# Where a scan's result is added up: row directions through TensorE and ScalarE, column directions on VectorE but later

## The chip, the cores and the metric

The kernel runs on one core of one Trainium2 chip. The metric is the device time of one execution in microseconds; lower is better. A core has five engines that each run their own queue of instructions in order: TensorE (PE, with its weight loads shown as PEld), VectorE (DVE), ScalarE (ACT), GpSimd (POOL) and SyncE (SP, which here only issues DMAs). They meet through semaphores.

## The reference

Two layers on an input of 4 images of 48 x 48 positions with 128 channels, all in float32. The part that matters here is the four-direction selective scan of the first layer:

```python
x0 = xc.reshape(B, d, L)
x1 = jnp.transpose(xc, (0, 1, 3, 2)).reshape(B, d, L)
xs = jnp.stack([x0, x1, x0[..., ::-1], x1[..., ::-1]], axis=1)
...
def step(h, inp):
    dt_l, u_l, B_l, C_l = inp
    dA = jnp.exp(dt_l[..., None] * A)
    h = h * dA + (dt_l * u_l)[..., None] * B_l[:, :, None, :]
    y = jnp.einsum('bkdn,bkn->bkd', h, C_l)
    return (h, y)
...
ys = ys + Ds.reshape(1, K, d, 1) * xs
y = ys[:, 0] + ys[:, 2][..., ::-1]
y1 = ys[:, 1] + ys[:, 3][..., ::-1]
y = y + jnp.transpose(y1.reshape(B, d, W, H), (0, 1, 3, 2)).reshape(B, d, L)
```

There are d = 256 inner channels and 16 states each; direction k = 0 goes along rows, 1 along columns, 2 and 3 are these backwards. The four results are added up. A layer normalisation, a gate and a projection follow. The second layer is an attention over the 2304 positions of each image and then a spectral filter ("stu"): 16 fixed filters `phi` are convolved with the sequence and mixed by matrices.

## The kernel before

**Stages.** The images are worked one after another. For each image there is a scan stage, and then a stage with epilogue (normalisation, gate, projection), attention and the next image's prologue (input projection, depthwise 3 x 3 filter). Ahead of the first image the prologue runs alone, with `weights` (loading and preparing the second layer's constants) threaded between its tasks. The spectral filter of image b runs on TensorE during the scan stage of image b + 1; that of the last image runs alone at the end, in another form. Image 0's scan stage has in its place `mixture`, which prepares the filter's matrices.

**The order is written out by hand**: the scheduler is off, and every engine runs its instructions in the order in which the Python code emits them.

**The scan stage.** `scans` runs over 192 units: 24 chunks (4 directions x 6 chunks of 384 positions), for each the 2 halves h of the inner channels and 4 groups q of states. A unit's tile `s` is 128 partitions (32 channels x 4 states) x 4 x 384. The life of unit u, one step of the loop per unit:

- `enter` (L517): s = dt*u times B, on VectorE for 5 units of 8 and on GpSimd for 3.
- `decay` (L526): ScalarE computes exp(dt*A) into one of the slots of `ring` in PSUM (4 slots for images 1 to 3). `fill`, called ahead of each scan, issues as many decays as there are free slots. Other short uses of PSUM (L438, L441, L509) take slots of the same ring.
- `scan` (L533): four scans a unit on VectorE; each frees its slot.
- `times_c` (L543): s times C, on GpSimd, in the next step.
- `sum_c` (L551): TensorE sums the 4 states of a channel with the matrix `csum` and accumulates the four q in one PSUM tile `ch.y`. It is emitted at the end of a step, for the two units of two and three steps before.
- `add_y` (L561, L563), one step after the last `sum_c` of a chunk's half: y is added to the image's sum `yaccs` (tiles `ya`, 128 x 48 x 48). In image 0, `sum_c` lets TensorE add the old content of `ya` to the same PSUM tile through an identity matrix (L554), and ScalarE copies the result back to `ya` (L561). In images 1 to 3 VectorE adds y to `ya` (L563). `in_order` gives the view of `ya` for a chunk: contiguous for row directions (even k), with a stride of 48 for column directions (odd k). `ch.y` has one buffer.

Between the four scans of a step, `more` emits work of the filter on TensorE by a budget of matmul columns (a share of the stage's total), so that its matmuls are spread evenly over the steps. In the filter (`stu`), three convolutions a filter (L1207) go through two PSUM banks, `cx` and `cy`; ScalarE copies them out (L1223, L1227, L1230, L1231), and L1273 multiplies by the mixing matrices. Each bank is written again only when its copy is done.

**The constants.** `weights` computes the differences of the filters, `fc` (L913 to L917), on 16 partitions x 1408 elements with three VectorE operations, and ScalarE's queue stores them to `fd`. They lie between the first tasks of the prologue, in which GpSimd computes a power (L243) for the normalisation that VectorE then applies (L245).

Of the kernel before, what the change touches and what calls it, by code (L numbers as in the profile page):

```python
# [10 lines left out]
ALU = mybir.AluOpType  # L11
# [13 lines left out]
G4, DL, C4, Q4 = 4, 32, 4, 4  # L25
# [35 lines left out]
def hybrid_kernel(ctx: ExitStack, tc: tile.TileContext, a: dict, out: bass.AP):  # L61
# [3 lines left out]
    nc = tc.nc  # L65
# [431 lines left out]
    class Unit:  # L497
# [47 lines left out]
        def sum_c(self, ps):  # L545

            ch = self.ch
            if self.q == 0:
                ch.y = ps.tile([P, 512], F32, tag="y", name=f"y{self.name}")
            for g in range(G4):  # L550
                nc.tensor.matmul(ch.y[g * DL:(g + 1) * DL, :CS], csum, self.s[:, g], start=(self.q == 0),  # L551
                                 stop=(self.q == Q4 - 1))
            if ch.b == 0 and self.q == Q4 - 1:
                nc.tensor.matmul(ch.y[:, :CS], ident, in_order(yaccs[ch.b][self.h], ch.k, ch.lo, CS), start=False,  # L554
                                 stop=True, skip_group_check=True)

        def add_y(self):
            ch = self.ch
            v = in_order(yaccs[ch.b][self.h], ch.k, ch.lo, CS)
            if ch.b == 0:  # L560
                nc.scalar.copy(v, ch.y[:, :CS].rearrange("p (r w) -> p r w", w=v.shape[2]))  # L561
                return
            nc.vector.tensor_tensor(v, v, ch.y[:, :CS].rearrange("p (r w) -> p r w", w=v.shape[2]), ALU.add)  # L563
# [53 lines left out]
    def scans(b, chunks, preps, front, sp, back, ring, finish, work, work_cols):  # L617

        units = [Unit(ch, h, q) for ch in chunks for h, q in quads]
        total = len(chunks) * CHUNK_COLS + work_cols  # L620
        done = [0]

        def more(share):

            while done[0] < share * total:
                cols = next(work, None)
                if cols is None:
                    break
                done[0] += cols

        def enter(s):

            if s + 2 < len(units) and units[s + 2].pool:
                units[s + 2].enter(sp.s, ring)
            if 0 <= s + 1 < len(units) and not units[s + 1].pool:
                units[s + 1].enter(sp.s, ring)

        wanted, issued = [], [0]

        def fill(left=0):  # L640

            while wanted and ring.free:
                wanted.pop(0).spread(ring)
            while len(ring.free) > left and issued[0] < G4 * len(units):
                i = issued[0]
                issued[0] += 1
                units[i // G4].decay(i % G4, ring)

        def scan(s, g):
            fill()  # L650
            units[s].scan(g, ring)

        def spread(s):
            if s < len(units) and not units[s].pool:
                wanted.append(units[s])

        def prepare(s):

            ci, j = divmod(s, len(quads))
            for c in range(ci + 1, ci + 5):  # L660
                if c < len(chunks) and 0 <= s - len(quads) * c + LEAD[c % 2] < STEPS[c % 2]:
                    done[0] += next(preps[c]) or 0

        def refill(s, i):

            if 0 <= s < len(units) and s // len(quads) + 1 < len(chunks):
                u, nxt = units[s], chunks[s // len(quads) + 1]
                if u.h == NH - 1:
                    nxt.fetch(i + u.q, front)

        pending = []
        spread(0)
        fill(len(ring.free) - 1)
        enter(-2)
        enter(-1)
        spread(1)
        fill(1)
        for i in range(3 if units[0].ch.b else 0):
            done[0] += next(work)
        for s in range(len(units) + 2):  # L680
            real = s < len(units)
            enter(s)
            prepare(s)
            if real:
                scan(s, 0)
            more((s + 0.25) / len(units))
            next(finish, None)
            if 1 <= s <= len(units):
                units[s - 1].times_c(s >= len(units) - (units[0].ch.b == 0))
            if real:  # L690
                scan(s, 1)
            if pending:
                pending.pop().add_y()
            prepare(s)
            more((s + 0.5) / len(units))
            next(finish, None)
            spread(s + 2)
            if real:
                scan(s, 2)
            more((s + 0.75) / len(units))  # L700
            next(finish, None)
            prepare(s)
            if real:
                scan(s, 3)
            refill(s - 2, Q4)
            refill(s + 1, 0)
            if s >= 2 and units[s - 2].q % 2:
                units[s - 3].sum_c(back.psy)
                units[s - 2].sum_c(back.psy)
                done[0] += 2 * CS  # L710
                if units[s - 2].q == Q4 - 1:
                    pending.append(units[s - 2])
            more((s + 1) / len(units))
            next(finish, None)
        for u in pending:
            u.add_y()
        for _ in work:
            pass
# [167 lines left out]
    def weights(one):  # L886

        def load(name, shape, src):  # L890
            t = one.tile(shape, F32, name=name)
            nc.scalar.dma_start(t, src)
            return t

        lg = load("lg", [P, NF], a["log_weights"].partition_broadcast(P))
        gu = load("gu", [P, NF], a["gumbel"].partition_broadcast(P))
        sg = load("sg", [P, KF], a["sigma"].partition_broadcast(P))
        ph = load("ph", [KF, 2, 2, LF + P + 1], a["phi"])
        mu = load("mu", [P, NF, 3, C], a["M_u"].rearrange("i j d e -> d i j e"))
        for i in range(6):  # L900
            yield
        hard, wts = [one.tile([P, NF], F32, name=n) for n in ("hard", "wts")]
        m = one.tile([P, 2], F32, name="m")

        nc.vector.tensor_add(lg, lg, gu)
        nc.vector.tensor_reduce(m[:, 0:1], lg, AX.X, ALU.max)
        nc.vector.tensor_scalar(lg, lg, m[:, 0:1], None, ALU.subtract)
        nc.scalar.activation(lg, lg, AF.Exp)
        yield

        fc = one.tile([KF, 3, 2, LF + P], F32, name="fc")
        n = LF + P
        nc.vector.tensor_copy(fc[:, 0], ph[:, :, 0, :n])  # L913
        yield
        nc.vector.tensor_sub(fc[:, 2], ph[:, :, 1, 1:], ph[:, :, 0, :n])
        yield
        nc.vector.tensor_sub(fc[:, 1], ph[:, :, 1, :n], ph[:, :, 0, :n])  # L917
        nc.scalar.dma_start(fd, fc)
        yield
        nc.vector.tensor_reduce(m[:, 0:1], lg, AX.X, ALU.add)  # L920
        nc.vector.reciprocal(m[:, 0:1], m[:, 0:1])
        nc.vector.tensor_scalar_mul(lg, lg, m[:, 0:1])
        nc.vector.tensor_reduce(m[:, 0:1], lg, AX.X, ALU.max)
        nc.vector.tensor_scalar(hard, lg, m[:, 0:1], None, ALU.is_equal)
        nc.vector.memset(m[:, 1:2], 1.0)
        yield
        for i in range(NF):

            nc.vector.tensor_tensor(hard[:, i:i + 1], hard[:, i:i + 1], m[:, 1:2], ALU.mult)
            nc.vector.tensor_tensor(m[:, 1:2], m[:, 1:2], hard[:, i:i + 1], ALU.subtract)  # L930
        nc.vector.tensor_sub(wts, hard, lg)
        nc.vector.tensor_add(wts, wts, lg)
        yield

        quarter = one.tile([P, KF], F32, name="quarter")
        nc.vector.memset(quarter, 0.25)
        nc.gpsimd.tensor_tensor(sg, sg, quarter, ALU.pow)
        mum = one.tile([P, NF, 3, C], F32, name="mum")
        nc.vector.tensor_scalar_mul(mum[:, NF - 1], mu[:, 0], wts[:, 0:1])
        for i in range(1, NF):  # L940
            nc.vector.tensor_scalar_mul(mum[:, NF - 1 - i], mu[:, i], wts[:, i:i + 1])
            nc.vector.tensor_tensor(mum[:, NF - 1 - i], mum[:, NF - 1 - i], mum[:, NF - i], ALU.add)
            yield
        nc.scalar.dma_start(mud, mum)
        for i in range(NF):
            nc.vector.tensor_scalar_mul(ws[:, :, i], sg, wts[:, i:i + 1])
        zero = one.tile([P, 4, 1], F32, name="zero")
        nc.vector.memset(zero, 0.0)
        nc.scalar.dma_start(ud[:, :, 0:1], zero)
# [817 lines left out]
```

## Time and profile before

| | us |
|---|---|
| median of 3 runs | 5428.56 (5426.13 to 5433.8) |
| profiled execution | 5427.03 |
| its span, first to last instruction | 5425.3 |
| scans of image 0 | 111.9 to 1059.3 |
| scans of image 1 | 1295.4 to 2250.8 |
| scans of image 2 | 2486.6 to 3442.2 |
| scans of image 3 | 3677.9 to 4633.2 |
| granted TensorE clock, mean (scan stage of image 0) | 0.926 (0.73) |

Times in the profile are microseconds from the first instruction of one profiled execution, unless marked ns. A group of instructions is one source line on one engine with its tiles, out<-in. A waits row names the engine and line that sat idle and, after the arrow, who ended the wait. A matmul in float32 stands in the profile as two instructions, and the ends of matmuls are modelled.

The busy share of the span in 40 equal slices, in tenths (9 is 90% or more), shows the alternation of the stages: four scan stages with VectorE at 9, and between them stretches in which TensorE leads.

```profile
PE   4555555599999999998899999898899999989999
...
DVE  8999999856999999856999999658999999423211
ACT  3666666546777766456776766457777666432111
POOL 2999999713989999605999999407998999201100
PEclk7777777799999999999999999999999999999999
```

### The profile page before, as it was taken

Reading aid. Unit: us, or ns where it says so; the run is one execution under the profiler, and the core shown is the slowest. Engines: PE = TensorE matmul, PEld = TensorE weight load, DVE = VectorE, ACT = ScalarE, POOL = GpSimd, SP = SyncE. Lnnn points to the kernel's source line nnn. Section 1 sums busy time; section 2 is a strip of 40 time slices with the busy share of each in tenths; the row PEclk is TensorE's granted clock in tenths of the full one; section 3 lists DMA queues with packets and bytes.
Section 4 is the critical chain, followed back from the end, with each engine's and each line's share of the span. In section 5 each row is a group of like instructions: output and inputs, shape, how many; then the busy total and the mean of one; then the engine's idle time right before and its main releaser. Section 6 shows DMA issues by size and latency. Waiting matters only on the chain. (4 is left out here: it accounts for less than half of the span.)

```text
span 5425.3 us, 71267 instructions
## 1 busy us (share of the span) xinstructions
PE 4658.1 (86%) x23372; PEld 3120.5 (58%) x23372; DVE 4324.9 (80%) x5309; ACT 3210.7 (59%) x6846; POOL 3656.8 (67%) x1881
## 2 busy tenths in 40 slices
PE   4555555599999999998899999898899999989999
PEld 2222222255666666645666666656666667559987
DVE  8999999856999999856999999658999999423211
ACT  3666666546777766456776766457777666432111
POOL 2999999713989999605999999407998999201100
PEclk7777777799999999999999999999999999999999
DMA  4444454404877777406787787227777777136543
GB/s 138 154 162 155 160 171 160 128 27 145 247 260 253 252 260 244 146 31 204 237 264 249 243 272 247 88 78 211 248 246 260 248 260 238 38 83 153 151 142 91
DMA packets 732185, 996.11 MB, mean 184 GB/s; under 512 B 108969, under 2 KB 580649, under 8 KB 731753
## 3 DMA queue, kind: packets, MB, share of 16 engines
q1 hardware_dynamic: 725992, 988.26, 57.6%
q10 hardware_dynamic: 5824, 3.30, 0.3%
q8 instruction: 187, 3.06, 0.2%
q14 instruction: 182, 1.48, 0.1%
HBM read 873.03 MB, written 118.31 MB: 183 GB/s over the span
## 5 line engine op out<-in xcount | busy, mean ns | idle before, releaser
L533 DVE TENSOR_TENSOR_SCAN s<-ring,s 128x385 f32<-128x385 f32 x3072 | 2691.4, 937 | 75.8 <-ACT ring L526 75.4
L543 POOL TENSOR_TENSOR s<-s,bc 128x1536 f32<-128x1536 f32 x763 | 2423.2, 3178 | 96.3 <-DVE s L533 39.9
L526 ACT ACTIVATE ring<-rep,A 128x384 f32<-128x384 f32 x3072 | 1757.8, 584 | 885.5 <-DVE s L517 524.2
L517 POOL TENSOR_TENSOR s<-rep,bc 128x1536 f32<-128x1536 f32 x288 | 994.2, 3452 | 131.9 <-DMA rep<-dtdud 70.9
L517 DVE TENSOR_TENSOR s<-rep,ring 128x1536 f32<-128x1536 f32 x480 | 830.3, 1731 | 34.9 <-ACT ring L509 20.0
L551 PE MATMUL y<-s,csum 128*32 128x384 f32 x6144 | 646.9, 538 | 109.4 <-POOL s L543 88.9
L1207 PE MATMUL cx<-tt,u 128*128 128x252 f32 (+7 forms) x2880 | 622.5, 361 | 124.3 <-ACT cy L1223 123.3
L1207 PEld LDWEIGHTS cx<-tt,u 128*128 128x128 f32 x2880 | 514.9, 195 | 308.0 <-ACT cy L1223 181.3
L1207 PE MATMUL cx<-tt,us 128*128 128x252 f32 (+7 forms) x2880 | 597.6, 352 | 51.5 <-ACT U L1231 49.4
L1207 PEld LDWEIGHTS cx<-tt,us 128*128 128x128 f32 x2880 | 494.6, 191 | 172.6 <-ACT U L1231 73.0
L1207 PE MATMUL cy<-tt,u 128*128 128x252 f32 (+5 forms) x2880 | 588.2, 349 | 0.0
L1207 PEld LDWEIGHTS cy<-tt,u 128*128 128x128 f32 x2880 | 497.2, 192 | 102.6 <-issue 41.1
L984 PE MATMUL G<-M,W 128*128 128x256 f32 (+3 forms) x512 | 222.7, 570 | 259.5 <-ACT W L974 134.7
L551 PEld LDWEIGHTS y<-s,csum 128*32 128x32 f32 x6144 | 166.3, 116 | 457.6 <-issue 259.0
L1273 PE MATMUL pr<-U,G 128*128 128x288 f32 (+4 forms) x1344 | 425.6, 448 | 3.0 <-DMA G<-gd 3.0
L1543 POOL TENSOR_TENSOR t<-s,s 128x512 f32<-128x512 f32 x48 | 63.4, 1320 | 513.8 <-ACT s L1541 513.8
L866 ACT ACTIVATE e<-s,shift 128x512 f32<-128x512 f32 (+1 forms) x360 | 230.2, 643 | 272.1 <-PE s L864 271.7
L864 PE MATMUL s<-xnT 128*128 128x512 f32 (+1 forms) x720 | 339.7, 556 | 23.7 <-ACT xnT L824 12.5
L856 PE MATMUL o<-e,xn 128*128 128x512 f32 (+1 forms) x720 | 336.9, 552 | 0.0
L984 PEld LDWEIGHTS G<-M,W 128*128 128x128 f32 x512 | 111.4, 239 | 364.0 <-ACT W L974 142.1
L1273 PEld LDWEIGHTS pr<-U,G 128*128 128x128 f32 x1344 | 235.0, 192 | 121.8 <-issue 71.4
L541 POOL COPY carry<-s 128x4 f32<-128x4 f32 x640 | 121.0, 189 | 231.9 <-DVE s L533 229.5
(237 smaller groups left out, 5040.6 us busy)
## 6 DMA issues: line engine op xcount, KB each, us to landing
rep<-dtdud SPq DMA_DIRECT2D x768, 384.0 KB
bc<-xdd SPq DMA_DIRECT2D x768, 192.0 KB
tt<-fd SPq DMA_DIRECT2D x144, 577.0 KB
tt<-fd SPq DMA_DIRECT2D x144, 451.0 KB
tt<-fd SPq DMA_DIRECT2D x144, 325.0 KB
dtdud<-dt SPq DMA_DIRECT2D x192, 192.0 KB
dtdud<-dx SPq DMA_DIRECT2D x192, 192.0 KB
t<-fd SPq DMA_DIRECT2D x80, 384.0 KB
```

Of the source, the lines that this page charges most:

```text
L517: eng.tensor_tensor(s, self.ch.rep[self.h][:, :, 1], bt.unsqueeze(1).to_broadcast([P, G4, CS]), ALU.mult)
L526: nc.scalar.activation(ring.body(self.dA[g]), ch.rep[self.h][:, g, 0], AF.Exp, scale=A[:, ch.k, self.h * G4 + g, self.q:self.q + 1])
L533: nc.vector.tensor_tensor_scan(s, ring.decays(i, ch.rev), s, 0.0, ALU.mult, ALU.add)
L541: nc.gpsimd.tensor_copy(carry[:, self.h, self.q].unsqueeze(2), self.s[:, :, end:end + 1])
L543: eng.tensor_tensor(self.s, self.s, ch.bc[Q4 + self.q].unsqueeze(1).to_broadcast([P, G4, CS]), ALU.mult)
L551: nc.tensor.matmul(ch.y[g * DL:(g + 1) * DL, :CS], csum, self.s[:, g], start=(self.q == 0), stop=(self.q == Q4 - 1))
L856: nc.tensor.matmul(po[J][:, :w], xn[:, i], e[:, :w], start=(i == 0), stop=(i == NT - 1))
L864: nc.tensor.matmul(p[:, :w], xnT[:, i * P:(i + 1) * P], xnT[:, 512 * J:512 * J + w], start=True, stop=True)
L866: nc.scalar.activation(e[:, :w], p[:, :w], AF.Exp, bias=shift)
L984: nc.tensor.matmul(p[:, :n], W[:, q if t else 0, i], M[t][:, i].unsqueeze(1).to_broadcast([P, n, C]), start=(t == 0 and i == 0), stop=(t = ...
L1207: nc.tensor.matmul(p4[:, 1:3, v - (hi - at):] if g else p4[:, 0:4:3, v - (hi - at):], x, t[:, :, hi - 1 - at + J * P:end if end >= 0 else ...
L1273: nc.tensor.matmul(o if q else o.rearrange("p f r m -> p r f m"), G, U[n][:, 4 * q:4 * q + 4, v0:v1].rearrange("p (a b) m -> p a b m", a=2 ...
```

## The change

The edits:

- `sum_c` and `add_y`: the path through TensorE and ScalarE, which image 0 has in all directions, is also taken by the row directions (even k) of images 1 to 3. Their column directions stay on VectorE.
- `scans`: in images 1 to 3 the pending `add_y` of a step is emitted after the fourth scan, not after the second. In image 0 it stays after the second.
- `weights`: the copy and the two differences of `fc` are GpSimd operations.

```diff
@@ sum_c
-            if ch.b == 0 and self.q == Q4 - 1:
+            if self.q == Q4 - 1 and (ch.b == 0 or ch.k % 2 == 0):
                 nc.tensor.matmul(ch.y[:, :CS], ident, in_order(yaccs[ch.b][self.h], ch.k, ch.lo, CS), start=False,
                                  stop=True, skip_group_check=True)
@@ add_y
-            if ch.b == 0:
+            if ch.b == 0 or ch.k % 2 == 0:
                 nc.scalar.copy(v, ch.y[:, :CS].rearrange("p (r w) -> p r w", w=v.shape[2]))
                 return
             nc.vector.tensor_tensor(v, v, ch.y[:, :CS].rearrange("p (r w) -> p r w", w=v.shape[2]), ALU.add)
@@ scans
             if real:
                 scan(s, 1)
-            if pending:
+            if pending and not units[0].ch.b:
                 pending.pop().add_y()
             prepare(s)
...
             if real:
                 scan(s, 3)
+            if pending:
+                pending.pop().add_y()
             refill(s - 2, Q4)
@@ weights
-        nc.vector.tensor_copy(fc[:, 0], ph[:, :, 0, :n])
+        nc.gpsimd.tensor_copy(fc[:, 0], ph[:, :, 0, :n])
         yield
-        nc.vector.tensor_sub(fc[:, 2], ph[:, :, 1, 1:], ph[:, :, 0, :n])
+        nc.gpsimd.tensor_tensor(fc[:, 2], ph[:, :, 1, 1:], ph[:, :, 0, :n], ALU.subtract)
         yield
-        nc.vector.tensor_sub(fc[:, 1], ph[:, :, 1, :n], ph[:, :, 0, :n])
+        nc.gpsimd.tensor_tensor(fc[:, 1], ph[:, :, 1, :n], ph[:, :, 0, :n], ALU.subtract)
```

Over the whole kernel that makes 72 additions fewer on VectorE (24 in each of three images), 72 identity matmuls more on TensorE and 72 copies more on ScalarE.

## The prediction

> **What bounds the kernel.** I read the page's first two parts, then the groups of instructions by line, then the stretches of busy time by stage, and last the waits inside one stage. The change works in two places: the prologue (first 30 us) and the scan stages of images 1, 2 and 3. In the trace the scans of image 1 run from 1295.4 to 2250.8, and the last addition of its y starts at 2254.2. Images 2 and 3 repeat the stage almost to the tenth of a microsecond, so one is worked out and taken three times.
>
> ```profile
> 1295.40:2254.50 959.10, 893.09 (x5047) 637.98 (x5047) 924.52 (x995) 681.88 (x1502) 875.58 (x428) 0.97 0.75 241
> 2486.60:3445.90 959.30, 892.94 (x5047) 638.06 (x5046) 924.52 (x995) 681.97 (x1502) 875.70 (x428) 0.97 0.75 241
> 3677.90:4637.00 959.10, 893.25 (x5047) 637.89 (x5047) 924.67 (x995) 681.95 (x1502) 872.48 (x425) 0.97 0.76 244
> ```
>
> The columns are the stretch, its length, then busy time of PE, PEld, DVE, ACT and POOL, the granted clock, and DMA. VectorE (DVE) is busy 924.5 of 959.1 us (96%), TensorE (PE) 893.1 (93%), GpSimd 875.6 (91%), ScalarE 681.9 (71%). VectorE is the pacer, and TensorE is three points behind it. The waits of the same stretch tell how each spends its idle time:
>
> ```profile
> DVE s L533 <- ACT ring L526: 21.5, 18, 4.2
> DVE ya L563 <- PE y L551: 10.2, 13, 1.9
> ...
> PE cx L1207 <- ACT cy L1223: 40.7, 26, 5.7
> PE cx L1207 <- ACT U L1231: 16.4, 12, 2.9
> ...
> ACT ring L526 <- DVE s L517: 126.7, 93, 4.7
> ACT ring L526 <- DVE s L533: 76.0, 190, 2.5
> ```
>
> Each row gives total us, times, longest. VectorE's 34.6 us of idleness are decays that come late (21.5) and y that TensorE has not finished (10.2). TensorE's 66 us of idleness are almost all waits for ScalarE's copies of the filter's banks (57.1). ScalarE itself waits 203 us for VectorE to free a slot of the ring, and those copies stand behind such decays in its queue. So a good part of TensorE's wait is only TensorE being ahead of VectorE. How large a part is the question on which this forecast turns.
>
> The stage in its four directions, k = 0 to 3 (rows, columns, rows backwards, columns backwards):
>
> ```profile
> 1295.40:1553.00 257.60, 228.93 (x1334) 166.84 (x1333) 242.49 (x270) 196.33 (x461) 225.97 (x113) 0.96 0.79 239
> 1553.00:1792.00 239.00, 222.05 (x1269) 158.94 (x1268) 233.67 (x248) 171.51 (x371) 219.16 (x107) 0.97 0.77 252
> 1792.00:2030.00 238.00, 228.34 (x1265) 161.03 (x1262) 229.48 (x249) 166.07 (x358) 219.82 (x107) 0.99 0.78 255
> 2030.00:2254.50 224.50, 213.76 (x1189) 151.17 (x1188) 218.88 (x232) 147.97 (x315) 210.64 (x104) 0.97 0.65 218
> ```
>
> TensorE's idle time is 28.7, 17.0, 9.7 and 10.7 us. Where the second row direction runs (k = 2), TensorE (228.3) and VectorE (229.5) are equally full, and there the change adds to TensorE.
>
> **What the skill's pages say.** The Trainium skill's "Perfetto Trace Analysis", section "Identifying the Most-Contended Engine", says that the matmul row's busy share does not tell how near TensorE is to its limit, and that the share of the weight loads should be read instead. That is 638 of 959 us here, 67%, which would leave a third of TensorE free. The trace speaks for less: outside the listed waits one matmul starts as the last one ends, so I go by the 66 us of gaps. The second page is "GPSIMD Engine Reference", section "3.1 Elementwise — side-by-side cycle accounting": the same elementwise operation of two inputs takes 1.96 times as long on GpSimd as on VectorE. In the trace the same product over 1536 elements takes 3.178 us on GpSimd and 2.025 us on VectorE (both L543), 1.57 times, so the direction agrees and the size does not. I scale from the trace's row.
>
> **The change, part by part** (for one image, unless said).
>
> *Row additions leave VectorE.* Of 48 additions an image, 24 are in row directions. The first 12, by line, against the 12 of the next, column direction:
>
> ```profile
> L563 DVE TENSOR_TENSOR ya<-ya,y x12: 520/534/555, 1327.9 to 1553.0; 128x384 f32<-128x384 f32 x12
> ...
> L563 DVE TENSOR_TENSOR ya<-ya,y x12: 805/830/864, 1570.4 to 1792.2; 128x384 f32<-128x384 f32 x12
> ```
>
> The group's mean of 684 ns mixes two prices; what is removed is the cheap half: 24 x 0.537 = 12.9 us. With them go VectorE's waits for y ahead of the row additions: 1.9 us in k = 0 and 3.4 in k = 2, together 5.3.
>
> *Column additions move two scans later.* Their order on VectorE changes and their number does not. Their waits today are 1.5 us (k = 1) and 3.6 (k = 3). Two scans are 1.9 us, and none of the waits but the very last of the stage (1.6) is longer than 1.5, so all go but that one, which is drained after the loop as before. Gain 1.5 + 2.0 = 3.5 us. The y bank is freed two scans later. Its next writer comes a full step after the addition's step (a step is 959/192 = 5.0 us), and TensorE reaches it about half a step behind VectorE, so nobody waits for it.
>
> VectorE's relief is 12.9 + 5.3 + 3.5 = 21.7 us: 8.3 in k = 0, 1.5 in k = 1, 9.9 in k = 2, 2.0 in k = 3.
>
> *TensorE gets 24 identity matmuls.* Image 0 has them, at a clock of 0.73. Nearer is a matmul of the same shape in this stage:
>
> ```profile
> L561 ACT COPY ya<-y x11: 470/472/478, 139.8 to 335.6; 128x384 f32<-128x384 f32 x11
> ...
> L438 PE MATMUL ring<-xd,dtw x84: 483/486/590, 1312.1 to 2122.4; 128*128 128x384 f32 x84
> ```
>
> A matmul stands as two instructions, and by the timeline a pair takes 0.645 us from its start to that of the next matmul. So 24 x 0.645 = 15.5 us, 7.7 in each row direction. Bounds: 0.5 us if the two passes hide the weight load, 0.9 if the latency shows (the timeline has a pair of 0.91 us). The matmul waits for the previous writer of its rows, one direction earlier, so never in fact.
>
> *ScalarE gets 24 copies* of 0.472 us (first row above), 11.3 us, in 277 us of idleness. In its queue each stands behind the decay that takes the slot of the step's third scan, and ahead of filter copies and the next decays. It waits only if y and the identity matmul come later than that: y was 0.9 us late or more at the old place twice in 24, and the new place is some 1.5 us later, with 0.65 of matmul ahead of it. About 1 us of blocking an image. Cover for a decay held up is the ring's other slots, up to three scans (2.8 us); without that cover each copy would cost its 0.47 us, 11 us in all. I add 1.3 us of new decay waits in k = 0, where today's are longest.
>
> *Prologue.*
>
> ```profile
> 20.23 1.61 DVE L915 TENSOR_TENSOR fc<-ph 16x1408 f32<-16x1408 f32 x1
> ...
> 24.93 1.61 DVE L917 TENSOR_TENSOR fc<-ph 16x1408 f32<-16x1408 f32 x1
> ```
>
> VectorE sheds 0.82 + 1.61 + 1.61 us. On GpSimd a difference is 1408/1536 x 3.178 = 2.9 us, the copy between 1.4 and 2.9. The copy and the first difference stand ahead of the power (L243) that the normalisation waits for. GpSimd is free from 16.5, so they end between 20.8 and 22.5; the power ran at 21.99, and with VectorE relieved could run at about 21.4. That is -0.6 to +0.6, say 0. The last difference stands behind the power, ends about 25.5 and releases the store in ScalarE's queue (today at 26.57), where the copies to xpad wait. VectorE runs without a gap from 24.93 to the first filter tap at 33.19, so its 1.61 us is gained. Image 0's own scans are unchanged: their addition stays where it was. Prologue: -1.6 us.
>
> **How much of the relief TensorE lets through.** In k = 0 TensorE needs 228.9 + 7.7 = 236.6 of 257.6 - 8.3 = 249.3 us, 95%, about what k = 2 runs with today: VectorE still sets the pace, gain 8.3 - 1.3 = 7.0. In k = 1 gain 1.5. In k = 2 TensorE needs 228.3 + 7.7 = 236.0, while VectorE could be through in 238.0 - 9.9 = 228.1: TensorE decides, and with 2 us of idleness left the direction lasts 238 as before, gain 0 (from -3 with half of today's waits left, to +2 with none). In k = 3 gain 2.0. Sum 10.5 us an image, 31.5 for three, 33.1 with the prologue. The profiled execution took 5427.0 (span 5425.3 and 1.7 around it), the median is 1.5 above it: 5427.0 - 33.1 = 5393.9, against the median 5428.6 - 33.1 = 5395.
>
> **Rivals.** *All the relief arrives*: if TensorE's waits were slack altogether and the lag of k = 2 is made up in k = 3, 3 x 21.7 + 1.6 = 66.7, time 5362. For it: ScalarE's 203 us of waits for VectorE ahead of the copies. Against it: in k = 2 there is no room for it.
>
> *TensorE becomes the bound (slower).* If the 57 us of waits for filter copies are the round trip from TensorE to ScalarE and back, they stay whatever VectorE does, and 24 matmuls lengthen every stage: 3 x 15.5 - 1.6 = +45, time 5473. It decides from the point where more than 959.1 - 893.1 - 15.5 = 50.5 us of today's 66 us idleness remain; between 29 and 50 part of the gain stays. For it: ScalarE waited for the filter's matmuls 50 us in 51 places in this stage, so the trip is not hidden everywhere. Against it: the longest of TensorE's waits (5.7 us) cannot be a copy of 0.5 us; ScalarE was held up by VectorE.
>
> *The two cancel*: some 45 to 50 us of idleness remain; the time lies within 11 us of before, about 5428.
>
> That the change does not do what it says is excluded by the order of instructions: 72 additions fewer on VectorE, 72 identity matmuls and 72 copies more.
>
> **Chances.** A part of the relief, 5395, own range 5376 to 5416: 0.53. All of it, about 5362: 0.13. Cancelled: 0.13. Slower, 5440 to 5473: 0.21. A difference of 0.2% (11 us) is what can be told from none, so faster 0.66, same 0.13, slower 0.21. The range runs from 5358 to 5450, which leaves out the worse part of the slower case and a little below the full relief.
>
> **What would show it.** After the change VectorE's wait for y should be near 2 us an image, TensorE's for the filter copies near 35 instead of 57, its share over 96%, and k = 2 should last about 238 us while k = 0 lasts about 250. I am wrong if TensorE's waits for copies stay at 57 (then slower), if k = 2 shrinks to 230 (then near 5362), or if VectorE's wait for decays grows past 32 us an image because ScalarE stands at its copies waiting for y.

## The result, and the profile after

The changed kernel takes 5450.14 us (median of 6 runs, 5442.39 to 5454.1) against 5429.46 us (6 runs, 5426.13 to 5433.8): 1.0042 times as long, 95% interval 1.0031 to 1.0053. It is slower by about 21 us, where 33 us of gain were forecast. The profiled execution took 5449.15 us with a span of 5447.4, 22.1 more than before. Of these, the scans of images 1 to 3 account for 23.1 (8.2, 6.4 and 8.5). The start was 4.7 us shorter, the stretches between the stages 5.7 longer and the tail 2.0 shorter.

The page's sum by engine, and the stretches of the changed kernel: first the whole stage of image 1 up to its last addition, then its directions k = 0 to 3, here cut exactly at their first scans (stretch, its length, busy PE, PEld, DVE, ACT, POOL, clock, DMA).

```profile
PE 4686.2 (86%) x23516; PEld 3146.2 (58%) x23516; DVE 4293.9 (79%) x5234; ACT 3237.6 (59%) x6918; POOL 3666.4 (67%) x1884
...
1290.30:2257.00 966.70, 904.28 (x5095) 647.13 (x5093) 914.76 (x970) 690.50 (x1526) 876.69 (x428) 0.97 0.74 239
...
1290.70:1542.20 251.50, 225.84 (x1301) 164.82 (x1301) 226.96 (x246) 192.41 (x454) 216.14 (x108) 0.95 0.78 237
1542.20:1780.30 238.10, 220.72 (x1275) 158.76 (x1273) 234.40 (x249) 171.77 (x371) 219.63 (x107) 0.99 0.77 250
1780.30:2022.50 242.20, 234.63 (x1279) 165.03 (x1276) 223.72 (x237) 169.92 (x367) 219.48 (x107) 0.98 0.77 253
2022.50:2254.30 231.80, 221.01 (x1237) 158.04 (x1237) 227.49 (x241) 156.40 (x334) 218.74 (x108) 0.99 0.66 221
```

Cut in the same way, the kernel before has 246.8, 239.8, 237.5 and 231.2 us. The two row directions, k = 0 and 2, became 4.7 and 4.8 us longer; the column directions changed by -1.8 and +0.6. Images 2 and 3 agree (k = 2 in image 2 has +3.2). VectorE's work fell as intended: in k = 2 it is busy 223.7 us instead of 229.1. But its idle time, length less busy, grew from 8.5 to 18.5 us there, and from 15.1 to 24.5 in k = 0. The relief arrived on the engine and did not shorten the stage.

The waits of the changed kernel in this stage (engine and line that waited, who ended the wait, total us, times, longest):

```profile
DVE s L533 <- ACT ring L526: 37.0, 27, 5.3
DVE s L517 <- issue: 5.5, 6, 1.6
DVE s L517 <- ACT ring L509: 5.3, 3, 4.1
```

```profile
PE cx L1209 <- ACT cy L1225: 36.9, 23, 6.1
PE cx L1209 <- ACT U L1233: 14.9, 10, 2.9
```

```profile
ACT ring L526 <- DVE s L517: 119.5, 86, 4.7
ACT ring L526 <- DVE s L533: 57.7, 170, 3.0
ACT U L1232 <- PE cx L1209: 35.3, 32, 4.8
ACT cy L1225 <- PE cx L1209: 26.6, 22, 3.6
ACT U L1229 <- PE cy L1209: 11.2, 13, 2.0
...
ACT ya L561 <- PE y L554: 0.4, 1, 0.4
```

(Lines of the filter and behind it stand two lower in the changed file: L1209 is L1207 of before.) VectorE's waits for y are gone, as forecast. What grew is its wait for decays, from 21.5 to 37.0 us. ScalarE's new copies do not stand waiting for y: the last row has them waiting 0.4 us in all. ScalarE waits 73.1 us for the filter's matmuls (three rows) where it waited some 50 before, and decays stand behind those copies in its queue. So TensorE is late, although it still idles 62.4 of 966.7 us. Its lateness is only a part of the growth: `after_no_matmul`, below, has no identity matmul in this stage, ScalarE waits 52.2 us for the filter there, and VectorE still waits 31.6 us for decays.

The new operations themselves cost what was assumed (minimum/median/maximum in ns of the matmul, and of the copy):

```profile
L554 PE MATMUL y<-ya,ident x48: 486/538/590, 1322.7 to 2031.6; 128*128 128x384 f32 x48
```

```profile
L561 ACT COPY ya<-y x24: 469/472/490, 1332.3 to 2034.2; 128x384 f32<-128x384 f32 x24
```

### The profile page after: what moved, and what is told of

It reads as the page before. It is cut to its first block, busy times and chain, and to the rows that moved or that the text cites. A ratio compares the mean times of both kernels' runs of the same rounds, so it can differ in the third digit from the quotient of the medians.

```text
span 5447.4 us, 71633 instructions
## 1 busy us (share of the span) xinstructions
PE 4686.2 (86%) x23516; PEld 3146.2 (58%) x23516; DVE 4293.9 (79%) x5234; ACT 3237.6 (59%) x6918; POOL 3666.4 (67%) x1884
## 5 line engine op out<-in xcount | busy, mean ns | idle before, releaser
L543 POOL TENSOR_TENSOR s<-s,bc 128x1536 f32<-128x1536 f32 x763 | 2424.3, 3181 | 96.8 <-DVE s L533 44.2
L1209 PE MATMUL cx<-tt,u 128*128 128x252 f32 (+7 forms) x2880 | 615.6, 358 | 111.5 <-ACT cy L1225 110.8
L1209 PEld LDWEIGHTS cx<-tt,u 128*128 128x128 f32 x2880 | 514.4, 195 | 282.6 <-ACT cy L1225 161.1
L1209 PE MATMUL cx<-tt,us 128*128 128x252 f32 (+7 forms) x2880 | 604.0, 355 | 46.7 <-ACT U L1233 44.5
L1209 PEld LDWEIGHTS cx<-tt,us 128*128 128x128 f32 x2880 | 502.1, 194 | 160.6 <-ACT U L1233 66.0
L1209 PE MATMUL cy<-tt,u 128*128 128x252 f32 (+5 forms) x2880 | 583.2, 347 | 0.0
L1209 PEld LDWEIGHTS cy<-tt,u 128*128 128x128 f32 x2880 | 495.9, 191 | 95.3 <-issue 32.4
```

The source lines that it names most:

```text
L543: eng.tensor_tensor(self.s, self.s, ch.bc[Q4 + self.q].unsqueeze(1).to_broadcast([P, G4, CS]), ALU.mult)
L1209: nc.tensor.matmul(p4[:, 1:3, v - (hi - at):] if g else p4[:, 0:4:3, v - (hi - at):], x, t[:, :, hi - 1 - at + J * P:end if end >= 0 else ...
```

## The experiments

"Before" is always the kernel before, run beside it on the same chip (5425.96 to 5429.63 us). Diffs are against the kernel before unless said.

**Which part of the change costs.** The change was split into its parts. `rows_only` has the first two hunks (`sum_c`, `add_y`), `later_only` the two in `scans`, `fc_only` the three in `weights`.

> Of the change only the later place of the addition, in images 1 to 3; all additions stay on VectorE. Theory A (the identity matmuls overload TensorE): this edit is harmless and takes away nearly all of VectorE's wait for y, 10.2 us an image down to about 2, so 3 x 8.6 = 26 us faster, about 5404. Rival B (the later place itself delays what follows the fourth scan): slower than before by 10 us or more, 5440 and up.

> Of the change only the row directions through TensorE and ScalarE, at the old place of the addition. Theory A: this alone holds the loss; without the help of the later place it is slower than the whole change, 5455 to 5475. Rival B: with the old place the loss is gone, 5395 to 5415.

> Of the change only the filters' copy and differences on GpSimd. By the trace of the changed kernel image 0's scans started 3.0 us earlier: 2 to 4 us faster than before, 5421 to 5424. Rival (the start is hidden behind later waits): no difference.

| run | us | before | ratio (95%) |
|---|---|---|---|
| later_only | 5426.54 | 5426.62 | 0.9998 (0.9990 to 1.0006) |
| rows_only | 5447.28 | 5426.62 | 1.0035 (1.0022 to 1.0047) |
| fc_only | 5425.86 | 5427.35 | 0.9996 (0.9988 to 1.0005) |

The loss lies in the row additions. The later place, expected to give 26 us, and the filters' differences give nothing that can be measured. `fc_only` also missed what was expected of it: image 0's scans began at 112.7 us there, 111.9 before and 108.9 in the changed kernel, so the earlier start of the changed kernel is not due to that edit. `later_only`, which leaves the prologue as it is, had 108.0: the start differs by that much from one profiled execution to another.

**The matmul or the copy.** `before_zero_matmul` leaves the addition on VectorE and adds a matmul with zero weights at the changed kernel's place:

```diff
-            if ch.b == 0 and self.q == Q4 - 1:
-                nc.tensor.matmul(ch.y[:, :CS], ident, ...
+            if self.q == Q4 - 1 and (ch.b == 0 or ch.k % 2 == 0):
+                nc.tensor.matmul(ch.y[:, :CS], zeros if ch.b else ident, ...
```

`after_no_matmul` is the changed kernel without the identity matmul in images 1 to 3 (`if self.q == Q4 - 1 and ch.b == 0`).

> The kernel before, with 24 more matmuls an image on TensorE at the same place (zero weights, so nothing is added); VectorE still adds, ScalarE copies nothing new. Theory A: TensorE's load alone makes it slower, 10 to 15 us an image, 5460 to 5475. Rival C (ScalarE's 24 copies hold up the decays): TensorE had 66 us of idle time, no change, 5425 to 5437.

> The changed kernel without the identity matmuls of images 1 to 3: ScalarE copies y over the image's sum, so the row directions' earlier content is left out. Theory A: the whole relief of VectorE arrives, about 3 x 21 + 3 us below before, 5360 to 5375. Rival C (ScalarE's copies are to blame): hardly better than the changed kernel, 5435 to 5450.

`before_zero_matmul`: 5454.51 us, 1.0047 (1.0035 to 1.0060). `after_no_matmul`: 5426.51, 0.9999 (0.9991 to 1.0007). So two things are shown. The matmuls alone cost the kernel before 28 us, more than the whole loss. And without them VectorE's relief, with ScalarE's 24 copies an image in place of the additions, is worth nothing, where 50 us or more were expected. A kernel with neither the additions nor the copies was not run, so what the copies take back of the relief is not known.

The two losses take different ways. In `before_zero_matmul` VectorE still adds y, and the matmul delays y: its waits for y are 19.6 us in the stage of image 1, where they were 8.6, and its waits for decays are as before (21.4). In the changed kernel no wait for y is left, and the loss comes through the decays.

**The same matmul at another place.** 24 matmuls an image, one a chunk, were added to the kernel before with VectorE's additions left alone: in `zero_step5` at the end of the sixth of a chunk's eight steps, in `zero_step7` at the end of the last (steps are counted from 0).

```diff
+            if ch.b and (self.h, self.q) == (0, 3):    # zero_step5; (1, 1) in zero_step7
+                nc.tensor.matmul(ch.y[:, :CS], zeros, yaccs[ch.b][self.h]...[:, :CS], start=False, ...)
```

> The kernel before with one matmul of zero weights in each of 24 chunks an image (all four directions), emitted at the end of the chunk's step 5, which TensorE reaches while VectorE is in the light steps. Theory A (TensorE's total load and its round trips with ScalarE set the pace in every step): about as the 24 in row directions alone, slower by 6 to 10 us an image, 5445 to 5457. Theory D (each step lasts as long as the slower of TensorE and VectorE in that step, and TensorE is the slower one only in light steps): the same, 5445 to 5460.

> The same 24 matmuls of zero weights an image at the end of step 7, ahead of the steps in which VectorE has most to do and TensorE idles most (about 2.5 us a chunk in k = 0). Theory D: hidden, less than 3 us an image, 5427 to 5436. Theory A: as at step 5, 5445 to 5457.

`zero_step5`: 5456.89 us, 1.0053 (1.0040 to 1.0065). `zero_step7`: 5431.94, 1.0012 (1.0004 to 1.0021). The same 72 matmuls cost 30.9 us at one place, 0.43 us each, and 6.0 us at the other, 0.08 each. The difference stands in one wait. VectorE's waits for y in the stage of image 1, before, in `zero_step5` and in `zero_step7`:

```profile
DVE ya L563 <- PE y L551: 8.6, 12, 1.9
```

```profile
DVE ya L568 <- PE y L556: 13.7, 17, 2.2
DVE ya L568 <- PE y L553: 5.4, 4, 3.0
```

```profile
DVE ya L568 <- PE y L553: 9.2, 13, 1.9
```

The 10.5 us more in `zero_step5`, three times, are its whole loss. Two things differ between the places: how far TensorE is behind, and how soon y is needed, for the addition on VectorE comes one step after step 5 and three steps after step 7. The forecast's sums by direction could see neither. Cut by step, from the starts of the first scans of units, k = 2 looks like this (mean us of a step over images 1 to 3; the steps left out differ by at most 0.05):

| kernel | step 2 | step 6 | step 7 | all eight |
|---|---|---|---|---|
| before | 5.89 | 5.82 | 7.39 | 39.59 |
| before, TensorE idle | 0.02 | 0.00 | 0.37 | 1.69 |
| changed | 6.01 | 5.61 | 8.15 | 40.28 |
| after_no_matmul | 5.57 | 5.19 | 8.31 | 39.56 |
| zero_step5 | 6.07 | 6.09 | 7.44 | 40.07 |
| zero_step7 | 6.00 | 5.82 | 7.31 | 39.62 |

VectorE's steps last from 3.4 to 7.4 us, while the filter's budget gives TensorE about the same work in each, 39.59/8 = 4.95 us. So TensorE falls behind in the short steps, and in k = 2 it idles only in steps 7, 0 and 1 (0.37, 0.84 and 0.46 us; 0.02 at most in each of the others). The identity matmuls stand at the ends of steps 1 and 5, ahead of and inside the stretch without idle time, and push back everything behind them. `zero_step7` puts its matmul ahead of steps 0 and 1, and TensorE's idle time falls by 0.50 us a chunk; in `zero_step5` it does not fall. In k = 0 the picture is less clean: there these three steps hold 3.0 of TensorE's 4.7 us of idle time a chunk.

**The changed kernel with its matmul moved there.** `ident_first` begins the accumulation of y with the identity matmul instead of ending it, which puts it at the ends of steps 3 and 7:

```diff
+            if self.q == 0 and first:
+                nc.tensor.matmul(ch.y[:, :CS], ident, in_order(...), start=True, ...)
```

> The changed kernel with the identity matmul at the start of y's accumulation and not at its end, so that it is emitted at the ends of steps 3 and 7 and not of steps 5 and 1; the same work in all. Theory D (a matmul costs where TensorE's backlog against VectorE is largest, and nothing where TensorE is ahead): the half at step 7 costs 0.1 us each, the half at step 3 between 0.1 and 0.4, so about 5 to 10 us above before, 5428 to 5440. Theory A (only TensorE's total counts): as the changed kernel, 5443 to 5455.

5431.57 us against 5427.35, 1.0008 (1.0001 to 1.0014). Most of the loss is gone, by the place of 72 matmuls alone; no gain appears. No y is waited for on VectorE in these directions, so here the place counts without that wait. But half of these matmuls stand at the end of step 3, where TensorE has no idle time in k = 2, and all of them together cost 4.2 us: idle time at the place is not the whole rule.

**Pacing the filter.** Instead of moving the matmul, the filter's budget in `more` was shared out by VectorE's time in each step, in the kernel before, in the changed one, in `ident_first`, and (`paced_late`) in the kernel before with `fc` on GpSimd; in the last two for k = 1 to 3 only. The core of the edit:

```diff
+            if units[0].ch.b:
+                x = share * len(units) - 1e-6
+                s = min(int(x), len(units) - 1)
+                share = (took[s] + at[s][0] + (x - s) * at[s][1]) / took[-1] ...
```

> The kernel before with the filter's work given to the steps of images 1 to 3 in proportion to VectorE's own time in the step, not evenly. Theory D: both engines' waits shrink, 10 us an image or more faster, below 5400. Theory A: TensorE's total is unchanged and its waits for copies stay, within 8 us of before, 5419 to 5435.

> The changed kernel with the same pacing by VectorE's time. Theory D: the identity matmuls stand in steps that now hold less filter work, so most of the loss is gone, below 5430. Theory A: as the changed kernel, 5440 to 5455.

> The kernel before with the filters' differences on GpSimd, and with the filter's work given out by VectorE's time only in the directions k = 1 to 3; k = 0, whose small blocks lost by it, stays even. Theory D: 3 us an image from the directions k = 1 to 3 and 3 us of the prologue, about 5414. If pacing gains nothing there: 5422 to 5428.

> The changed kernel with the identity matmul first and the same pacing in k = 1 to 3. If VectorE's relief is worth something once TensorE's work stands where it has room: below the version with pacing alone by 10 us or more, 5405 or less. If VectorE does not set the pace (theory D): not faster than pacing alone, 5412 to 5430.

`paced_before` 5440.87 (1.0026, 1.0017 to 1.0035), `paced_after` 5437.82 (1.0018, 1.0012 to 1.0025), `paced_late` 5429.33 (1.0000, 0.9992 to 1.0009), `ident_first_paced` 5432.75 (1.0009, 1.0001 to 1.0017). None gained over before; `paced_after` shows about half of the changed kernel's loss. In k = 0 of image 1, `paced_before` took 253.8 us where before took 246.8; k = 2 fell by 1.5. Less backlog on TensorE is thus not by itself a gain, and something else holds the stage.

**Is it TensorE's total, or VectorE's and TensorE's together?** One of the mixing products was left out, which takes 44 us of TensorE's work out of each stage: in `before_less_pe` from the kernel before, in `relief_less_pe` from `after_no_matmul`.

```diff
-                for v0, v1, x in parts(w, extra):
+                for v0, v1, x in parts(w, extra) if q else ():
```

> The kernel before with one of the two mixing products (L1273, q = 0) of the filter of images 0 to 2 left out: some 70 us of TensorE's work an image less, the budget unchanged. If TensorE sets the pace of the scan stages: 15 to 25 us an image faster, down to VectorE's own floor of some 930 us a stage, 5350 to 5385. If VectorE sets it (as the prediction said): VectorE's waits alone can go, 10 us an image at most, 5397 to 5427.

> The same product left out, and VectorE relieved as in the changed kernel (ScalarE copies y in row directions, without the identity matmul, so the sum's earlier content is left out). With TensorE out of the way VectorE's 12.9 us an image should now show: 25 to 45 us below the run without the relief. If VectorE's relief is worth nothing even then, the decays on ScalarE or GpSimd set the pace: within 8 us of it.

`before_less_pe`: 5427.83 against 5426.51, 0.9998 (0.9990 to 1.0006). `relief_less_pe`: 5414.10, 0.9975 (0.9966 to 0.9985). In the kernel before, TensorE's total is not the bound. Taking VectorE's 12.9 us of additions (for copies on ScalarE) or TensorE's 44 us away gives nothing alone; both together give 12 us.

**Where the relief goes: step 7.** In `after_no_matmul`, steps 2 and 6 of k = 2 became 0.32 and 0.63 us shorter and step 7 became 0.92 longer: the relief is given back in step 7. Of the 0.92, 0.56 are later decays and 0.35 a longer dx. In k = 0, where step 7 grew by 0.58, it is 0.53 of later decays, and dx is unchanged.

**The decays of step 7.** In every second chunk ScalarE computes the softplus of dt for two later chunks there (L452), and the trace has a table load ahead of it and another ahead of the next decay, 4.2 us in which no decay is made. One such place in k = 0 of image 1, in the kernel before, with the scan that waits for the decay behind it (start, us, engine, line; in brackets the idle time before and who ended it):

```profile
1412.55 1.28 ACT L452 ACT_TABLE_LOAD   x1
1413.84 1.58 ACT L452 ACTIVATE dt<-dt 128x768 f32<-128x768 f32 x2
1415.44 1.28 ACT L526 ACT_TABLE_LOAD   x1
1416.73 0.58 ACT L526 ACTIVATE ring<-rep,A 128x384 f32<-128x384 f32 x1
```

```profile
1417.35 0.96 DVE L533 TENSOR_TENSOR_SCAN s<-ring,s 128x385 f32<-128x385 f32 x1 [1.28 <-ACT ring L526]
```

The same block and scan in `after_no_matmul`:

```profile
1411.30 1.28 ACT L452 ACT_TABLE_LOAD   x1
```

```profile
1416.10 0.96 DVE L533 TENSOR_TENSOR_SCAN s<-ring,s 128x385 f32<-128x385 f32 x1 [1.76 <-ACT ring L526]
```

Counted from the start of the block, VectorE is ready for this scan 0.48 us sooner and waits 0.48 us longer. In the stage of image 1, 17.5 of VectorE's 21.5 us of waits for decays follow such a block before, some 22 of 31.6 in `after_no_matmul`. Some of the other late decays of step 7 stand directly behind a new copy of y. No run moved the block, so this is read from the traces and not tested.

**The other side: VectorE against GpSimd.** The timeline of the kernel before in step 7 of the second chunk of k = 2, VectorE and GpSimd:

```profile
1855.33 3.17 POOL L543 TENSOR_TENSOR s<-s,bc 128x1536 f32<-128x1536 f32 x1
1857.89 1.50 DVE L474 TENSOR_TENSOR dx<-dt,xc 128x384 f32<-128x384 f32 x2
1859.32 0.95 DVE L533 TENSOR_TENSOR_SCAN s<-ring,s 128x385 f32<-128x385 f32 x1
...
1860.33 0.19 POOL L541 COPY carry<-s 128x4 f32<-128x4 f32 x1 [1.82 <-DVE s L533]
```

And the same place in `after_no_matmul`:

```profile
1852.68 3.18 POOL L543 TENSOR_TENSOR s<-s,bc 128x1536 f32<-128x1536 f32 x1
1853.30 3.44 DVE L474 TENSOR_TENSOR dx<-dt,xc 128x384 f32<-128x384 f32 x2
1856.67 0.95 DVE L533 TENSOR_TENSOR_SCAN s<-ring,s 128x385 f32<-128x385 f32 x1
...
1857.68 0.19 POOL L541 COPY carry<-s 128x4 f32<-128x4 f32 x1 [1.82 <-DVE s L533]
```

Two products dx (L474) take 1.50 us before and 3.44 us here; the shortest single one takes 0.53. The first of each pair ended 0.42 us after GpSimd's product (1858.92 against 1858.50; 1856.28 against 1855.86), and the second followed at once. In `after_no_matmul` VectorE came to dx earlier in GpSimd's product, and waited longer inside it. The trace repeats this: of the 44 dx in the stage of image 1 before, 12 were running when a product of GpSimd ended, and each ended 0.41 or 0.42 us after it, or 0.68 to 0.72 where it reads `xc` with a stride, however early it had begun. The other 32 took 0.87 us at most. The last scan of step 7 stands behind dx, and GpSimd waits for that scan: the 1.82 us in brackets here, some 2.5 us a chunk on average. These are most of its waits in the stage but one of 19.9 us, as its rows for the kernel before show:

```profile
POOL carry L541 <- DVE s L533: 57.6, 27, 6.9
POOL s L517 <- PE cx L1207: 19.9, 1, 19.9
POOL s L543 <- DVE s L533: 11.6, 6, 3.9
```

The time inside dx is listed in no view as a wait, because it is in dx's duration. In the row directions of the changed kernel itself, dx is no longer than before (in k = 0 of image 1 the twelve take 8.5 us in all against 9.4, in k = 2 8.9 against 9.2), so this is no part of its loss there.

The Trainium skill, "SBUF — State Buffer", section "Who interferes with whom", has the rule for it: a VectorE instruction with two inputs in SBUF and a GpSimd instruction that reads SBUF shut each other out for the whole instruction. To test it, `before_dx_psum` gives dx a constant in PSUM in place of `xc`, so one SBUF input is left; `relief_dx_psum` does that to `after_no_matmul`, and `relief_dx_less_pe` leaves out the mixing product too.

```diff
-                nc.vector.tensor_tensor(o, v, x, ALU.mult)
+                if isinstance(bank["mm"], Ring):    # in the scan stages; elsewhere the line above
+                    one = bank["mm"].t[0][:, 400:496].unsqueeze(1).to_broadcast([P, 4, 96])
+                    nc.vector.tensor_tensor(dx[:, h]..., dt[:, h]..., one, ALU.mult)
```

> The kernel before with one input of dx (L474) taken from PSUM in the scan stages (a constant there in place of xc, which is left out), so that it reads SBUF once. In the traces so far a long dx (up to 3.0 us, 0.53 alone) always ends some 0.5 us after a product of GpSimd ends. If VectorE has to wait there for GpSimd (theory E): all dx near 0.5 us, 8 to 14 us of VectorE's time an image less, and the total faster by up to that, 5385 to 5420. If the long ones have another cause: dx stays as long as it was, 5422 to 5430.

> The changed kernel without its identity matmuls (VectorE relieved, the sum's earlier content left out) and with the same dx. Theory E (the relief was lost because VectorE came sooner to a dx that waited longer): 15 us or more below the run before_dx_psum. If the relief is lost at the late decays instead: within 8 us of it.

> As the last, and with one of the filter's two mixing products left out too (some 45 us of TensorE's work an image less). If all three engines hold the stage by turns (each alone gave 0, relief and TensorE together gave 12 us): 10 to 25 us below relief_dx_psum. If TensorE has no part: within 8 us of it.

| run | us (before: 5426.82) | ratio (95%) | k = 0 to 3, image 1 |
|---|---|---|---|
| before_dx_psum | 5378.21 | 0.9912 (0.9898 to 0.9925) | 246.4, 237.1, 236.3, 226.2 |
| relief_dx_psum | 5365.17 | 0.9888 (0.9874 to 0.9901) | 246.4, 233.4, 235.4, 226.2 |
| relief_dx_less_pe | 5362.00 | 0.9882 (0.9869 to 0.9896) | 244.9, 234.4, 232.7, 226.7 |

One small operand gives 48.6 us, more than was expected; 19.0 of them lie in image 0's stage. VectorE's relief on top of it (`relief_dx_psum`) gives 13.0 us, between the 15 or more of one theory and the 8 or less of the other, and 3.2 us come from less work on TensorE, which is no more than was expected if it has no part. Dx in k = 2, before and then in `before_dx_psum`:

```profile
L474 DVE TENSOR_TENSOR dx<-dt,xc x12: 530/666/1614, 1819.2 to 2016.3; 128x384 f32<-128x384 f32 x12
```

```profile
L477 DVE TENSOR_TENSOR dx<-dt,ring x12: 526/545/554, 1797.6 to 1993.0; 128x384 f32<-128x384 f32 x12
```

The long ones are gone. Two reservations: in column directions the edit also removes the strided read of `xc` (dx took 0.80 us at best there and takes 0.54 now), and the gain in image 1 is mostly theirs (2.7 and 5.0 us, against 0.4 and 1.2 in the row directions). So not all of the 48.6 us need be the lock. And the row directions remain stubborn: k = 2 falls by 4.9 us or more in every image only when dx, the additions and TensorE's work are all lightened (with dx alone by 3.7 in image 3 and 1.2 or 1.3 in the others), and k = 0 never falls by more than 2.5.

**Moving dx.** `dx_last` keeps all work and puts dx behind the last scan of step 7:

```diff
-            prepare(s)
             if real:
                 scan(s, 3)
+            prepare(s)
```

> The kernel before with the third preparation of a step (in step 7 of a chunk it is dx of the next chunk) put behind the step's last scan in place of ahead of it; the amount of work is the same. Theory of the loop (GpSimd's product holds up dx, dx holds up the last scan of step 7, and GpSimd waits some 2.5 us a chunk for that scan): GpSimd no longer waits for dx, 0.4 to 0.9 us a chunk are gained over 96 chunks, 5340 to 5390 us. Rival: dx, now behind the scan, waits for the whole of GpSimd's next product (3.2 us) and the scans of step 0 wait for dx: no gain, or slower, 5425 to 5480 us.

5434.48 us against 5429.63 (13 and 17 runs), 1.0007 (0.9998 to 1.0015): no gain, the rival's side. Half of the loop's premise held: GpSimd's wait for that scan fell from some 2.5 to some 1.2 us a chunk. But now dx meets the next product, and GpSimd its turn to wait. The dx, and GpSimd's small copy, in the stage of image 1 of `dx_last`:

```profile
L474 DVE TENSOR_TENSOR dx<-dt,xc x44: 531/798/3809, 1332.5 to 2173.8; 128x384 f32<-128x384 f32 x44
```

```profile
L541 POOL COPY carry<-s x160: 178/189/842, 1292.6 to 2212.0; 128x4 f32<-128x4 f32 x160
```

Before, the longest dx of that stage was 2.28 us and the longest copy 0.21. GpSimd's busy time in the stage rose by 18.4 us (872.7 to 891.0) and its idle time fell by 14.8: the collision was moved, not removed.

## Why the prediction was wrong, step by step

- **"VectorE is the pacer"** is the step that failed. Its 96% were true and did not name the bound: 12.9 us of additions an image and the waits for y taken away, with copies on ScalarE for them, gave nothing (`after_no_matmul`). What is saved in steps 2 and 6 is lost again in step 7, mostly in waits for decays and in k = 2 also in a longer dx; and some of VectorE's busy time was waiting inside dx.
- **The relief of 21.7 us an image** was delivered: no wait for y is left among VectorE's larger waits, and the additions are gone. Its forecast worth in k = 0, 7.0 us, was 0.3 (`after_no_matmul`, 246.5 against 246.8 us). In k = 2 it was 0.2. There the forecast had 0 for the whole direction, because TensorE would decide; the direction became 4.8 us longer.
- **The matmuls in k = 0** were taken as hidden, because 95% of TensorE would be used; with them the direction went from 246.5 to 251.5 us. **In k = 2** they were set against "2 us of idleness left", and the direction went from 237.3 to 242.3. Both are sums over a whole direction. In k = 2 TensorE's idle time lies in steps 7, 0 and 1, and the matmuls at the ends of 1 and 5. The price of a matmul was 0.08 or 0.43 us by its place, and no total shows that. The estimate of 0.645 us of TensorE a matmul was near: its busy time rose by 12.4 us for 24, 0.52 each, and from the start of such a pair to the next matmul it was 0.75.
- **The columns' later place**, 3.5 us an image: k = 1 gained 1.8 against the 1.5 forecast, k = 3 lost 0.6 against a gain of 2.0. Alone (`later_only`) it is worth nothing that can be measured.
- **ScalarE's copies hidden, 1 us of blocking**: right about the blocking; they waited 0.4 us. Yet "1.3 us of new decay waits" in k = 0 was 9.3 (11.1 to 20.4 us), and 5.2 of it is there without the identity matmuls (16.3 us in `after_no_matmul`). It is not ScalarE standing at y, as the last paragraph of the prediction would have had it: VectorE reaches the decays of step 7 sooner, and with the matmuls TensorE is late as well.
- **The prologue's 1.6 us** was not seen in `fc_only`.
- **What would show it**: TensorE's waits for copies are 51.8 us, neither 35 nor 57, and its share is 93.5%, not over 96. VectorE's wait for decays did pass 32 us (37.0), one of the signs of being wrong, though not for the reason given there.
- **The rival "TensorE becomes the bound"** was right in sign. Its test was even met, 62.4 us of idleness remaining where it asked for 50.5. Its mechanism was not: in the kernel before, a TensorE with 44 us less to do leaves the time as it is. The identity matmuls cost by their place in the step.
- **Readings.** The 2.025 us for VectorE's product (L543) is a mean of five: four took 1.76 us, and one took 3.09, begun while a product of GpSimd was running. So GpSimd's 3.178 is 1.81 times the undisturbed one and not 1.57, and the collision of the two engines stood in that row before the change was made. ScalarE's 50 us of waits for the filter's matmuls came in 54 places, not 51.

What stays open: what holds k = 0, where no combination brought more than 2.5 us while GpSimd, TensorE and VectorE each idle for 15 to 31 us (half of VectorE's 15.1, 7.8 us, follows ScalarE's softplus blocks, which no run moved); how much of the relief ScalarE's copies took back; how much of a matmul's price is TensorE's backlog and how much the nearness of what waits for it; and how the 48.6 us divide between the lock and the strided read. A dx that multiplies by the real `xc` with one operand in PSUM was not tried. No version that keeps the whole computation was measurably faster than the kernel before.

## What to carry to other kernels

In an order written by hand in which engines take turns, compare engines step by step and not by their totals: what added work costs depends on the idle time at its own place and on how soon its result is needed, and removed work is worth only what the next meeting point with another engine lets through. Before calling an engine the pacer because it is busy, compare the shortest and the longest duration of each of its operations; one that varies threefold, as dx does here, can be a wait in disguise. And when a wait is for another engine's result, look at what that engine was doing just then. An experiment that takes work away from the supposed pacer, ahead of the change, would have told in one run that the gain is not there.

## What the runs showed that had not been expected

- A VectorE product of 128x384 with two SBUF inputs takes 0.53 us alone and up to 2.28 us in image 1's stage before (3.81 in `dx_last`), when it meets a GpSimd product of 3.18 us, and then ends just after it; with one input in PSUM, k = 2 has 0.526 to 0.554. It works the other way as well: a copy of 0.19 us on GpSimd took up to 0.84 in `dx_last`.
- 72 equal matmuls cost 30.9 or 6.0 us by their place in an eight-step chunk.
- VectorE's 12.9 us (moved to ScalarE as copies) and TensorE's 44 us a stage were each worth nothing alone and 12 us over the kernel together.
- Most of VectorE's waits for decays, 17.5 of 21.5 us in the stage of image 1 before, follow 4.2 us of ScalarE in which a softplus stands between two table loads of 1.28 us each.
